# Two Mamba heads computed in pieces during attention's last blocks, and a hand-made order for the first units of the next layer

## The chip, the cores and the metric

The kernel runs on one core of a Trainium2 chip. The core has five engines that work side by side, each with its own instruction queue: TensorE (PE, matrix products; its weight loads are shown apart as PEld), VectorE (DVE), ScalarE (ACT), GpSimd (POOL) and SyncE (SP, which here only issues DMAs). An instruction starts when those ahead of it in its queue have started and the semaphores that it waits for have come. The metric is the device time of one execution in microseconds, the median of three runs.

## The reference

Four layers run over one image `x` of 2 x 64 channels x 96 x 96 pixels, L = 9216 pixels for each of two batch items.

```python
# layer 0: attention over all pixels, softmax not scaled
f = einsum('bnc,bcm->bnm', theta_x, phi_x)
y = einsum('bnm,bmc->bnc', softmax(f), g_x)
x = batchnorm(conv1x1(y)) + x
# layer 1: depthwise 3x1 and 1x3, 1x1 convolution, batch norm, relu,
#          then one Mamba over the L pixels of an item
seq = relu(bn(conv1x1(x + dwh(x) + dww(x))))
h = layernorm(seq)
xm, z = split(h @ in_proj.T)
xc = silu(causal_conv4(xm) + b)
dt, Bm, Cm = split(xc @ x_proj.T)          # 4, 16, 16
dt = softplus(dt @ dt_proj.T + dt_b)
h_t = exp(dt_t * A) * h_{t-1} + dt_t * B_t * xc_t     # 128 x 16 states
x = ((sum_s h_t C_t + xc * D) * silu(z)) @ out_proj.T + seq
# layer 2: four more Mambas along rows and columns, two directions each
# layer 3: a 3x3 filter made from the image's own channel means
```

Only the joint of layers 0 and 1 is touched.

## The kernel before

Channels lie on partitions: item 0 on rows 0 to 63, item 1 on 64 to 127. Two tiles, `xa` and `xb`, of 128 x 9216 float32 hold the image.

**Attention** is `layer0_direct`. For each item it makes `theta`, `phi` and `g` (the last in the lower half of `xb`) and then goes over 18 blocks of 512 queries, each in 18 groups of 512 keys. In a group PE makes two score tiles (`scores`, L302) while ACT turns the scores of that group into exponentials (`exps`, L316), PE multiplies those of the group before with `g` (`values`, L327), and DVE adds them up for the softmax's sums (L405, L414). Score tiles alternate between two PSUM buffers of two banks each (`f`); the banks `m` and `po` serve a block's `sums` (L349) and `project` (L362), which are done for the last block at groups 3 and 7 of the next. Small pieces of other work are hung into the groups by generators: weights of layer 1 in item 0 (`ready_weights`), and in item 1 the depthwise convolution of layer 1 (`convolution`, L192 and L201 on DVE), whose chunks of 768 pixels go to DRAM (`image1`, L183). It is done for eleven of twelve chunks. After the last block come `fold`, `sums`, `invert` and `project` with nothing beside them. Then a flag is loaded by all engines and a branch taken (L149): if a softmax sum was out of range, `layer0_general` does attention again in a safe form. In the measured runs it is skipped.

**Layers 1 and 2** are `layers1_2`. The scan over pixels is cut in units: 24 of layer 1 (2 items x 12 chunks of 768 pixels), then 96 of layer 2. A unit has a *head*: centring and layer norm (`norm_*`), the causal convolution with 4 taps (`conv`), the gate, Silu, the step width (`step_*`, which ends in four products that are summed by PE, `sum_mm`), and a write of step width and input to DRAM rows (`step_write`, L928). Then sixteen *steps*: 16 x 8 states of a group are spread over the partitions by DMA from those rows (`read`, L964, two DMAs of 384 KB each, into six buffers `spread`), ACT makes the decays (L987), DVE multiplies the inputs by B (L1000, into the PSUM tiles `place`) and scans (L1009 with a carried state in layer 1, L1014 in layer 2), POOL multiplies by C (L1016), PE gathers (L1027). C, B and the tail are further products. All products of heads and tails go through one pair of PSUM banks with tag `m` (`open`, `mm`), so that each must be read by ACT before the next may begin.

The order of all this is not left to a scheduler. The tables `CARRY` and `FRESH` give each operation a due time in steps, counted from its unit's first step, and `run` (L1211) sorts them all and issues them in that order, every engine's queue being filled in it. Units are 16 steps apart, and heads begin some 47 steps before their unit. The first unit is an exception: its head is issued whole at the start, together with the pointwise convolution of chunks 0 to 4 (`first`, L207 and L208), and the second unit is placed 32 steps after the first, one unit's length being left for its head:

```python
begin = self.STEPS * (i + (i > 0))
order += [(begin + when, u, name, args) for when, name, args in self.events(u) if i or not is_head((0, name))]
```

Before that, `layers1_2` issues all loads of the image chunks (L1272) and the depthwise convolution of the twelfth (L192, L201), from `xa`, which then becomes the room for small tables (`carver`). The pointwise convolutions of chunks 5 to 11 and the weights of layer 2 are made by a generator `other`, two of its pieces in each unit.

Of the kernel before, what the change touches and what calls it, by code (L numbers as in the profile page):

```python
# [19 lines left out]
FP = mybir.dt.float32  # L20
# [5 lines left out]
P = 128  # L26
B, C, H, W = 2, 64, 96, 96
L = H * W
# [44 lines left out]
def rows_of(b):  # L73
    return slice(b * C, (b + 1) * C)
# [62 lines left out]
    return scale, bias  # L137


def layer0(k, x, pre):  # L140

    nc, tc = k.nc, k.tc
    scale, bias = batch_norm(k, "bn0", "bn0_gamma", "bn0_beta", "bn0_mean", "bn0_var", "w_b")
    bad = layer0_direct(k, scale, bias, pre)
    with tc.If(nc.values_load(bad, min_val=0, max_val=1) > 0):  # L149
        nc.sync.dma_start(out=k.xa, in_=x)  # L150
        layer0_general(k, scale, bias)
        with tc.tile_pool(name="pre", bufs=2) as wp:
            for c in range(L // CH - 1):
                for _ in pre.chunk(c, wp):
                    pass


class Pre:
# [49 lines left out]
        self.nc.scalar.activation(part, whole, AF.Relu, bias=self.bias, scale=self.scale)  # L208


def layer0_direct(k, scale, bias, pre):


    nc, tc = k.nc, k.tc
# [6 lines left out]
    with (  # L221
# [121 lines left out]
        def fold(block):  # L343
            block.fold = wp.tile([P, NB], FP, tag="fold", bufs=1, name="fold")
            nc.gpsimd.tensor_add(block.fold, block.acc[:, :NB], block.acc[:, NB:])
# [24 lines left out]
        def convolutions():  # L370
            for c in range(L // CH - 1):
                while not ready or ready[-1] < pre.takes(c):
                    yield
                yield from pre.chunk(c, wp)

        ready_weights = prepare(k, att.tile([P, 640], FP, name="scratch"), product)
        convolution = convolutions()
        last = None
        for b in range(B):
            rows = rows_of(b)  # L380


            theta = att.tile([P, L], FP, tag="theta", name=f"theta{b}")
            phi = att.tile([P, L // 2], FP, tag="phi", name=f"phi{b}")
            g = k.xb[:, : KEYS * C].rearrange("p (m c) -> p m c", m=KEYS)


            sides = ((rows, k.xa[rows, : L // 2]), (rows_of(1 - b), k.xb[rows_of(1 - b), L // 2 :]))
            projections(theta, phi, g, sides)

            pending = None
            for i in range(NBLK):
                block = SimpleNamespace(rows=rows, i=i, acc=wp.tile([P, 2 * NB], FP, tag="acc", name="acc_e"))
                for n in range(NGROUP):
                    es = exps(scores(theta, phi, i, n))
                    if n == 3 and last:
                        sums(last)
                    if n == 7 and last:
                        project(last)
                        if last.rows == rows_of(B - 1):  # L400
                            ready.append((last.i + 1) * NB)
                    if n == 0:
                        nc.vector.tensor_add(block.acc, es[0], es[1])
                    else:
                        nc.vector.tensor_add(block.acc, block.acc, es[0])  # L405
                    if pending:
                        one, at, e = pending
                        if at == 0:
                            one.y = [bank("y0"), bank("y1")]
                        values(g, one.y, at, e)  # L410
                        if at == NGROUP - 1:
                            collect(one)
                    if n:
                        nc.vector.tensor_add(block.acc, block.acc, es[1])  # L414
                    if n == 0 and last:
                        fold(last)
                    if n == 3 and last:
                        invert(last)
                    pending = block, n, es
                    if b == 0 and (made or 5 <= n < NGROUP - 1):  # L420
                        made.clear()
                        next(ready_weights, None)
                    if b == B - 1:
                        next(convolution, None)
                last = block
            one, at, e = pending
            values(g, one.y, at, e)
            collect(one)
        fold(last)
        sums(last)  # L430
        invert(last)
        project(last)
        ready.append(L)
        for _ in convolution:
            pass
# [271 lines left out]
class Mamba:  # L707
# [37 lines left out]

    def open(self, name="mm"):

        return self.wide(self.ps_m.tile([P, 2 * NB], FP, tag="m", name=name))

    def half(self, sides, j, terms, rows=slice(0, P)):  # L750

# [37 lines left out]
    def norm_square(self, u):  # L789

        if u.carry:
            u.norm.x = self.work("xn", D_CONV - 1 + CH)
            u.sq = self.sq
            self.nc.scalar.activation(u.sq, u.p, AF.Square)
            self.nc.scalar.copy(u.norm.x[:, D_CONV - 1 :], u.p)  # L795
# [28 lines left out]
    def norm_scale(self, u):  # L824
        if u.norm.unit is not u:
            return
        nc = self.nc
        x = u.norm.x[:, D_CONV - 1 :]
        if u.carry:
            before = u.norm.x[:, : D_CONV - 1]  # L830
            if u.norm.before is None:
                nc.gpsimd.memset(before, 0.0)
            else:
                nc.gpsimd.tensor_copy(before, u.norm.before.x[:, CH:])
        nc.gpsimd.tensor_mul(x, x, u.sq)

    def norm_affine(self, u):
# [370 lines left out]
                add(s + table["shared"], "shared", *divmod(s // 4, PARTS))  # L1208
        return at

    def run(self, units, first, n_first, other, ending):  # L1211


        self.ending = (units[-1], ending)
        for u in units:
            u.dtu, u.h, u.decay, u.bx, u.C = {}, {}, {}, {}, {}
        self.nc.scalar.preload_act_table_set("natural_log_exp_and_others")
        first(0)
        heads = ("norm", "image", "conv", "gate", "silu", "step", "sum", "c")
        is_head = lambda e: e[1].split("_")[0] in heads  # L1220
        for _, name, args in sorted(filter(is_head, self.events(units[0])), key=lambda e: e[0]):
            getattr(self, name)(units[0], *args)
            if name == "norm_root":
                first(1)
            if name == "c_read_1":
                first(2)
        for c in range(3, n_first):
            first(c)
        order = []
        for i, u in enumerate(units):  # L1230
            begin = self.STEPS * (i + (i > 0))
            order += [(begin + when, u, name, args) for when, name, args in self.events(u) if i or not is_head((0, name))]
        for _, u, name, args in sorted(order, key=lambda e: e[0]):
            if name == "other":
                next(other, None)
            else:
                getattr(self, name)(u, *args)


def prepare(k, scratch_tile, product):  # L1240
# [9 lines left out]
    yield from mamba_weights(k, k.weights[0], k.const, product, 0)  # L1250


def layers1_2(k, pre, padded):

# [9 lines left out]
    with ExitStack() as stack:  # L1266
# [1 line left out]

        last = L // CH - 1
        FIRST = 5  # L1270
        for c in range(last):
            nc.sync.dma_start(out=k.xb[:, bass.ts(c, CH)], in_=pre.image[:, bass.ts(c, CH)])  # L1272

        for _ in pre.depthwise(last, k.xb[:, bass.ts(last, CH)]):
            pass

        def first(c):

            pre.pointwise(k.xb[:, bass.ts(c, CH)], *(m.places[c % 3] if c % 3 < 2 else m.open()))


        carver = Carver(k.xa)
        for _ in by_state(k, k.weights[0], carver, 0):
# [34 lines left out]

        def other():
            for c in range(FIRST, L // CH):  # L1320
                part = k.xb[:, bass.ts(c, CH)]
                sides, whole = m.open()
                for j, p in enumerate(sides):
                    rhs = part[:, bass.ts(j, HALF)]
                    nc.tensor.matmul(p, lhsT=k.mat("conv_w"), rhs=rhs, start=True, stop=True)
                yield
                nc.scalar.activation(part, whole, AF.Relu, bias=pre.bias, scale=pre.scale)
                yield
            for (which, lin_w, _), to in zip(layer2, joins):
                for i in which:  # L1330
                    yield from mamba_weights(k, k.weights[i], carver, m.product, i)
                yield from joined(which, lin_w, to)
# [17 lines left out]
        for (which, _, lin_b), to, order in zip(layer2, joins, ("p (t n) -> p n t", "p (n t) -> p n t")):  # L1350
            xs = k.xb.rearrange(order, n=W)
            for b in range(B):
                rows = rows_of(b)
                for n in range(0, W, SEQS):
# [12 lines left out]
                    pair[1].out.append((to[2][rows], half))  # L1367
                    pair[1].last, norm.unit = pair, pair[0]
                    units += pair
        m.run(units, first, FIRST, other(), padded.early)  # L1370


class Padded:
# [133 lines left out]
@with_exitstack  # L1507
def conv_seq_kernel(ctx: ExitStack, tc: tile.TileContext, x, cols, mats, dtw, out):
    k = setup(ctx, tc, x, cols, mats, dtw)
    dram = ctx.enter_context(tc.tile_pool(name="dram", bufs=1, space=bass.MemoryType.DRAM))  # L1510
    pre = Pre(k, dram)
    layer0(k, x, pre)
    padded = Padded(k)
    with tc.manual_schedule():
        layers1_2(k, pre, padded)
        layer3(k, padded, out)


# [79 lines left out]
```

## Time and profile before

| | us |
|---|---|
| runs | 7355.49, 7357.27, 7360.73 |
| median | 7357.27 |
| the profiled execution, its time | 7357.56 |
| its span | 7355.6 |
| last `y_one` copy of attention | 2378.99 |
| first operation after the branch | 2394.56 |
| one block of attention in item 1 | 64.18 |

| engine | busy us | share of the span |
|---|---|---|
| PE | 6315.5 | 86% |
| DVE | 6693.8 | 91% |
| ACT | 5484.4 | 75% |
| POOL | 4609.6 | 63% |

The page cuts the span into 40 slices of 184 us and gives each engine's busy share in tenths:

```profile
PE   9999999999999688887788778788787777777777
...
DVE  6788887888888499999999999999999999999999
ACT  5555555555555688887888888888888888888884
POOL 0000000000000489888899999999999999999996
PEclk9999999999999799999899999999999999999998
DMA  1000000000000466665677667677676766766764
```

A 9 is 90% or more. PEclk is the clock that PE was granted, in tenths of full speed. The fourteenth slice holds the joint of layers 0 and 1. In a timeline each line has a start, a busy time, the engine, the line of the code, the operation with its output and inputs, and how many instructions are merged; a bracket gives the idle time just before, and what ended it. A release is inferred from semaphores, and a wait for several is put down to the one that came last.

### The profile page before, as it was taken

To read this page: it belongs to the slowest core of one execution; us is meant where nothing else is said; L and a number is where in the kernel's file an instruction comes from. 1 tells how busy PE (TensorE), PEld (TensorE's weight loads), DVE (VectorE), ACT (ScalarE), POOL (GpSimd) and SP (SyncE) were. 2 spreads that over 40 slices of the span, in tenths; PEclk is the share of its full clock that TensorE was granted. 3 is DMA by queue.
4 is the path that set the end of the run, shared out by engine and by line. 5 is a ranking of instruction groups with operands and counts; after the bars stand their busy time and mean duration, and the time that the engine had idled before them with its cause. 6 is when DMAs were issued, how large, how long until landed. Compare 5 with 4: busy or idle time off the path is not lost.

```text
span 7355.6 us, 106020 instructions
## 1 busy us (share of the span) xinstructions
PE 6315.5 (86%) x38502; PEld 2351.6 (32%) x38502; DVE 6693.8 (91%) x5703; ACT 5484.4 (75%) x7902; POOL 4609.6 (63%) x3078
## 2 busy tenths in 40 slices
PE   9999999999999688887788778788787777777777
PEld 3333333333333233222233333233333333333333
DVE  6788887888888499999999999999999999999999
ACT  5555555555555688887888888888888888888884
POOL 0000000000000489888899999999999999999996
PEclk9999999999999799999899999999999999999998
DMA  1000000000000466665677667677676766766764
GB/s 47 1 1 1 1 1 1 3 6 6 6 6 6 123 163 169 164 170 155 176 182 183 180 178 183 176 184 181 181 183 177 185 182 175 187 182 176 186 180 129
DMA packets 301157, 878.11 MB, mean 119 GB/s; under 512 B 33608, under 2 KB 35660, under 8 KB 300112
## 3 DMA queue, kind: packets, MB, share of 16 engines
q1 hardware_dynamic: 300184, 869.94, 45.5%
q8 instruction: 303, 4.96, 0.3%
q14 instruction: 230, 1.88, 0.1%
q10 hardware_dynamic: 440, 1.32, 0.1%
HBM read 767.71 MB, written 103.42 MB: 118 GB/s over the span
## 4 chain that ended last, share of the span: by engine, by line
DVE 16%; issue 13%; PE 11%; ACT 7%; POOL 4%; DMA 2%; DVEq 0%; POOLq 0%; ACTq 0%; SPq 0%
DVE h L1014 9%; DVE place L1000 7%; PE mm L757 6%; POOL h L1016 3%; ACT h L987 2%; DMA spread<-rows 2%; PE conv L859 1%; PE y L1027 1%; PE B L992 1%; PE y L1022 1%; ACT raw L864 0%; DVE done L1487 0%; ACT raw L873 0%; ACT xa L821 0%; ACT raw L870 0%
## 5 line engine op out<-in xcount | busy, mean ns | idle before, releaser
L1016 POOL TENSOR_TENSOR h<-h,C 128x768 f32<-128x768 f32 x1920 | 3455.2, 1821 | 291.0 <-DVE h L1014 245.1
L1014 DVE TENSOR_TENSOR_SCAN h<-h,place 128x768 f32<-128x768 f32 x1344 | 2286.7, 1737 | 12.6
L316 ACT ACTIVATE e<-f_exp 128x1024 f32<-128x1024 f32 x1296 | 1257.8, 1022 | 984.7 <-PE f_exp L302 984.6
L987 ACT ACTIVATE h<-spread,rates 128x384 f32<-128x384 f32 x3408 | 1838.9, 606 | 10.8 <-DMA spread<-rows 9.1
L1000 DVE TENSOR_TENSOR place<-spread,B 128x768 f32<-128x768 f32 x1704 | 1546.0, 947 | 133.3 <-DMA spread<-rows 53.5
L1027 PE MATMUL y<-h,held 128*32 128x384 f32 x7680 | 1102.7, 514 | 380.7 <-POOL h L1016 379.9
L327 PE MATMUL y<-e,xb 64*64 64x512 f32 x10368 | 1232.1, 590 | 0.0
L302 PE MATMUL f_exp<-theta,phi 64*64 64x512 f32 x10368 | 1230.1, 589 | 2.0 <-DVE xb L287 1.4
L405 DVE TENSOR_TENSOR acc_e<-acc_e,e 128x1024 f32<-128x1024 f32 x612 | 771.3, 1260 | 298.1 <-ACT e L316 280.6
L341 POOL TENSOR_TENSOR ys<-ys,y_one 128x512 f32<-128x512 f32 x36 | 45.9, 1275 | 1455.9 <-DVE ys L340 1455.9
L414 DVE TENSOR_TENSOR acc_e<-acc_e,e 128x1024 f32<-128x1024 f32 x612 | 811.0, 1325 | 65.5 <-DVE acc_e L405 1.8
L992 PE MATMUL B<-raw,xa 128*128 128x384 f32 x960 | 490.4, 596 | 263.1 <-DVE place L1000 260.7
L1009 DVE TENSOR_TENSOR_SCAN h<-h,state,place 128x384 f32<-128x384 f32 x720 | 670.8, 991 | 2.4
L327 PEld LDWEIGHTS y<-e,xb 64*64 64x64 f32 x10368 | 393.7, 133 | 728.1 <-issue 722.7
L302 PEld LDWEIGHTS f_exp<-theta,phi 64*64 64x64 f32 x10368 | 395.3, 133 | 713.7 <-issue 701.9
L1027 PEld LDWEIGHTS y<-h,held 128*32 128x32 f32 x7680 | 212.6, 109 | 1151.9 <-POOL h L1016 761.8
L366 POOL TENSOR_TENSOR xa<-xa,t_att 64x512 f32<-64x512 f32 x36 | 54.5, 1514 | 756.6 <-ACT t_att L364 735.9
L757 PE MATMUL mm<-dtu,ident 128*128 128x384 f32 x960 | 427.1, 551 | 24.9 <-ACT xb L1065 14.5
L934 PE MATMUL mm<-raw,xa 128*128 128x384 f32 x960 | 376.2, 515 | 31.3 <-ACT xn L795 27.8
L1000 POOL TENSOR_TENSOR bx<-spread,xa 128x768 f32<-128x768 f32 x216 | 392.7, 1818 | 4.7 <-ACT xa L996 3.2
L992 PEld LDWEIGHTS B<-raw,xa 128*128 128x128 f32 x960 | 159.3, 207 | 578.2 <-DVE place L1000 412.6
L1014 DVE TENSOR_TENSOR_SCAN h<-place,bx 128x768 f32<-128x768 f32 x192 | 334.1, 1740 | 0.3 <-ACT place L987 0.3
(222 smaller groups left out, 7050.1 us busy)
## 6 DMA issues: line engine op xcount, KB each, us to landing
spread<-rows SPq DMA_DIRECT2D x1920, 384.0 KB, 6.1
rows<-dtu SPq DMA_DIRECT2D x120, 768.0 KB, 4.6
image<-pre SPq DMA_DIRECT2D x11, 384.0 KB, 2.3
xb<-image SPq DMA_DIRECT2D x11, 384.0 KB, 7.3
xa<-in_x SPq DMA_DIRECT2D x1, 2304.0 KB, 22.6
xa<-in_x SPq DMA_DIRECT2D x3, 384.0 KB, 11.3
xb<-in_x SPq DMA_DIRECT2D x3, 384.0 KB, 11.9
xa<-in_x SPq DMA_DIRECT2D x1, 1152.0 KB, 17.9
```

What stands on the lines that cost most here:

```text
L302: nc.tensor.matmul(f[rows_of(half), bass.ts(side, NB)], lhsT=phi[at, m * P + half * C : m * P + (half + 1) * C], rhs=theta[at, bass.ts(i, ...
L316: nc.scalar.activation(e, f, AF.Exp)
L327: nc.tensor.matmul(ys[half][rows_of(side)], lhsT=g[at, m, :], rhs=e[at, bass.ts(side, NB)], start=m < 2, stop=m >= KEYS - 2,)
L405: nc.vector.tensor_add(block.acc, block.acc, es[0])
L414: nc.vector.tensor_add(block.acc, block.acc, es[1])
L757: self.nc.tensor.matmul(o, lhsT=lhsT, rhs=x, start=n == 0, stop=n == len(terms) - 1)
L987: self.nc.scalar.activation(u.decay[step][:, q], dt[:, q], AF.Exp, scale=rate)
L992: self.nc.tensor.matmul(self.B, lhsT=u.w.bc[0][part], rhs=x, start=True, stop=True)
L1000: engine.tensor_mul(u.bx[step], self.spread(u, step, 1), B)
L1014: nc.vector.tensor_tensor_scan(*flat, 0.0, ALU.mult, ALU.add)
L1016: nc.gpsimd.tensor_mul(h, h, C)
L1027: self.nc.tensor.matmul(y, lhsT=self.t.gather[block // 4], rhs=u.h[step][:, q], start=False, stop=stop)
```

## The change

A new class `Early` computes the heads of the first two units of layer 1. Its generator `pieces` does pointwise convolution, layer norm, taps and gate for unit 0 and then unit 1, cut at each `yield`; `layer0_direct` takes a piece in each group from 9 to 16 of item 1's blocks from the fifth on, and further ones while a product is held in a bank (`yield True`). Products use the banks `m` and `po` by halves of 384 columns. The rest, Silu for both units and the step width of unit 0 up to its rows in DRAM, is issued between and after `fold`, `sums`, `invert` and `project`. Its tiles lie in the upper half of `xb`, which attention no longer needs in item 1. The branch's safe side does the same afterwards.

In `layers1_2` the chunk loads, the pointwise convolutions and the last chunk's depthwise convolution (`edge`) become events with due times, since the upper half of `xb` comes free only later. `run` leaves out the heads that are done, puts unit 1 at 2.5 steps behind unit 0's end (`GAPS`), gives the rest of its head times of its own (`SECOND`), and shortens the lead of unit 2's head by 0.85 (`FACTORS`). A new method `emit` walks the sorted events and holds one back while a tile or bank that it takes (`TAKES`) is not yet given back (`GIVES`). Eight products into an unread bank (`FILL_FIRST`) open the layer. A one-column Silu comes before the switch to the table set with Ln and Exp.

The diff, cut to its core:

```diff
+class Early:
...
+        for c, raw in enumerate(self.raw):
+            image, xc, gate = self.both[:, bass.ts(c, CH)], raw[:, :CH], raw[:, CH:]
...
+            nc.sync.dma_start(out=image, in_=pre.image[:, bass.ts(c, CH)])
+            yield
+            yield
+            ps = product(k.mat("conv_w"), image)
+            yield True
+            for j, p in ps:
+                nc.scalar.activation(part(image, j), p, AF.Relu, bias=pre.bias, scale=pre.scale)
+            yield
+            yield
+            ps = banks()
+            for j, p in ps:
+                nc.tensor.matmul(p, lhsT=k.tables.centre[own], rhs=part(image[own], j), start=True, stop=True)
+            yield True
...
+            for j, p in ps:
+                nc.scalar.activation(part(sq, j), p, AF.Square)
+                nc.scalar.copy(part(x, j), p)
+            yield
+            yield
+            ps = product(k.mean, sq, split=True)
+            yield True
+            for j, p in ps:
+                nc.scalar.activation(part(sq, j), p, AF.Ln, bias=k.eps)
+            nc.scalar.activation(sq, sq, AF.Exp, scale=-0.5)
+            yield
+            nc.gpsimd.tensor_mul(x, x, sq)
+            yield
+            nc.scalar.activation(x, x, AF.Identity, bias=k.col("ln_b"), scale=k.col("ln_g"))
...
+            yield self.REST if c else None
+        for raw in self.raw:
+            nc.scalar.activation(raw, raw, AF.Silu)
+        xc = self.raw[0][:, :CH]
+        nc.scalar.preload_act_table_set("natural_log_exp_and_others")
+        yield
+        ps = product(w.step, xc)
+        for j, p in ps:
+            nc.scalar.activation(e[:, j], p, AF.Abs, bias=w.dt_b)
+            nc.scalar.activation(dt[:, j], p, AF.Relu, bias=w.dt_b)
+        yield
+        nc.scalar.activation(e, e, AF.Exp, scale=-1.0)
+        nc.scalar.activation(kept, e, AF.Identity, bias=1.0)
+        nc.scalar.activation(kept, kept, AF.Identity, scale=-1.0, bias=1.0)
+        nc.scalar.activation(log, e, AF.Ln, bias=1.0)
...
+        nc.gpsimd.tensor_mul(e, dt, by_half(xc))
+        nc.sync.dma_start(out=self.rows, in_=self.both)
...
                     if b == B - 1:
                         next(convolution, None)
+                    if b == B - 1 and i >= 4 and held != Early.REST and (held or 9 <= n < NGROUP - 1):
+                        held = next(head, False)
...
         fold(last)
+        next(head)
         sums(last)
+        next(head)
         invert(last)
         project(last)
+        for _ in head:
+            pass
...
+        for i in range(self.fill):
+            self.nc.tensor.matmul(sides[i % 2], lhsT=k.ident, rhs=k.mats[:, :HALF], start=True, stop=True)
...
+    GAPS = (2.5, 0, 0)
+    FACTORS = (0.85, 1, 1)
...
+    FILL_FIRST = 8
+    FILL = 0
+    FILL_UNTIL = 3
+    LOADS = (-6.1, 2.3, 5.6, 8.7)
+    FIRST_1 = 11
...
         for i, u in enumerate(units):
-            begin = self.STEPS * (i + (i > 0))
-            order += [(begin + when, u, name, args) for when, name, args in self.events(u) if i or not is_head((0, name))]
+            begin = self.STEPS * i + sum(self.GAPS[:i])
...
+        for when, chunks in zip(self.LOADS, ((2,), (3,), (4, 0, 1), (5, 6, 7))):
+            when = min(when, *(firsts[c] - 1 for c in chunks if c in firsts), 100)
+            order.append((when, None, "load", load, chunks))
+        self.emit(sorted(order, key=lambda e: e[0]))
...
-        for c in range(last):
-            nc.sync.dma_start(out=k.xb[:, bass.ts(c, CH)], in_=pre.image[:, bass.ts(c, CH)])
-
-        for _ in pre.depthwise(last, k.xb[:, bass.ts(last, CH)]):
-            pass
...
             for c in range(FIRST, L // CH):
+                if c == FIRST + 1:
+                    load(8, 9)
+                if c == FIRST + 2:
+                    load(10)
+                    edge()
```

## The prediction

> **What bounds the kernel now.** I read the forty slices first: PE is at nine tenths up to about a third of the span, DVE from there to the end. The slices between are neither, and they are what the change touches. Stretches cut at the joints of the timeline give sizes:
>
> ```profile
> 2300.00:2350.00 50.00, 50.00 (x456) 17.38 (x452) 41.94 (x35) 28.54 (x30) 4.90 (x3) 1.00 0.00 1
> ...
> 2394.50:2453.00 58.50, 37.75 (x87) 16.61 (x88) 4.66 (x6) 27.98 (x35) 3.58 (x4) 0.70 0.38 119
> 2453.00:2496.40 43.40, 32.44 (x120) 12.88 (x122) 42.21 (x47) 33.30 (x51) 32.55 (x32) 0.73 0.45 104
> 2496.40:2533.00 36.60, 25.44 (x66) 9.48 (x62) 0.00 (x0) 16.89 (x20) 7.54 (x8) 0.72 0.61 151
> 2533.00:2576.40 43.40, 33.62 (x122) 13.57 (x122) 41.88 (x47) 35.96 (x57) 33.79 (x33) 0.80 0.53 137
> ```
>
> Columns: stretch, length, busy us of PE, weight load, DVE, ACT, POOL, granted clock, DMA share, GB/s. In attention PE has no idle time: work put there costs its full length. Then DVE works 4.7 us of 58.5 (unit 0's head is being made), 42 of 43.4 (unit 0), nothing for 36.6 (unit 1's head) and 42 of 43.4 again (unit 1). From there on DVE is about 98% busy (835 us of 2600 to 3450), so whatever brings the first two units forward reaches the end of the kernel. The timeline names the two stalls:
>
> ```profile
> 2382.39 1.13 PE L349 MATMUL m<-fold,ones 128*128 128x512 f32 x2 [3.49 <-POOL fold L345]
> ...
> 2389.82 0.77 ACT L364 ACTIVATE t_att<-po,bn_bias,bn_scale 64x512 f32<-64x512 f32 x1 [10.25 <-PE po L362]
> ...
> 2394.66 0.68 DVE L192 TENSOR_SCALAR xb<-xa,dw_centre,dw_b 128x768 f32<-128x768 f32 x1 [4.72 <-PEq L149]
> ...
> 2423.85 1.28 ACT L874 ACT_TABLE_LOAD   x1
> ...
> 2440.60 0.34 SPq L928 DMA_DIRECT2D rows<-dtu  x1
> ...
> 2452.97 1.83 DVE L1000 TENSOR_TENSOR place<-spread,B 128x768 f32<-128x768 f32 x2 [53.54 <-DMA spread<-rows]
> ...
> 2533.04 1.83 DVE L1000 TENSOR_TENSOR place<-spread,B 128x768 f32<-128x768 f32 x2 [36.69 <-PE B L992]
> ```
>
> **A. Pieces inside attention: +20 us.** Both heads up to the gate run in four or five of batch 1's blocks. Per unit PE gets five groups: pointwise (2 matmuls of 384 columns), centring (2, one row half, so one after the other), mean (2 halves side by side, as long as one), taps (8 in pairs, as 4), gate (as 1), together ten lengths. A length is about 0.64 us (L757 shows 0.81 for 2 records at full clock, of which the last part is drain). Each group also breaks attention's alternation. That price is in the trace: a block of 18 groups takes 64.18 us (distance of two L339 copies), a plain group 3.433, so the two inserted 512-column matmuls (L349, L362) cost 2.38, 1.19 each, of which 0.85 is streaming and 0.34 the break. Two units: 2 x (6.4 + 5 x 0.34) = 16.2 us, nothing beside it.
>
> ACT has 1.49 us idle of each 3.43 (the bracket before L316). In the timeline the pair of exps ends at 2373.18, and PE first needs their second bank again at 2374.43, 1.25 later, so ACT can take some 2.7 us more in one group before PE stalls. Relu, conv read, affine and gate (about 1.0 us each) and the squares and copies (about 1.9) fit. The root does not: two Ln halves (0.56 each, by the 384-column exps of L987), Exp 0.84, and two table loads, one to the set with Ln and one back. By the trace's row (1.28 us, the next ACTIVATE follows at once) that is 4.5 us, a stall of 1.8 per unit, 3.6 for both. The Trainium skill ("ScalarE: Activation LUTs", section "What ACT_TABLE_LOAD costs") says that a switch costs a drain of 1.38 us besides the 1.28 of the load. By it the root takes 7.3 us, stalls 4.5 per unit, and A is 25. The trace has no such gap around L873 and L874, so I take the row and keep 25 as the upper end; the lower end, no breaks and no stall, is 12.8. The two image loads in SP's queue are asked for two groups (6.9 us) before their matmul; an image write lands in 2.3 us alone. POOL is 8% busy there: its pieces cost nothing, and would cost only if later than their two groups.
>
> **B. Tail and unit 0: -32.5 us** (against 2452.97, without A's shift). After the last copy at 2379.6 ACT loads a table, does two Silus (1.48 each), loads back: 2385.2. PE does the sums first, then unit 0's step product, to 2386.4; Abs and Relu by halves end near 2387.5, under DVE's reciprocal and before `t_att` needs ACT (2389.8). So no cost to attention's own tail. Behind `t_att` (2390.6) come Exp, two Identities, Ln (3.4 us): 2394.0. The sums follow; the same tail, Ln's end to the last matmul, took 6.1 us before at the low clock: 2400. Copy 0.5, POOL product 1.8, rows write issued 2402.5; issue to the first read was 3.9 us before: 2406.4. The branch now stands behind all this on PE; its compare took 3.8 us after a 0.5 us load, so PE goes on at 2404.4 instead of 2394.6, beside the write.
>
> Two things now release unit 0's first DVE operation. Data: reads from 2406.4, with the small weights and one image load before them, first spread 6 to 8.5 us later, 2413 to 2415. PE: its new order puts eight filling matmuls, chunk 2's pointwise, unit 2's centring and unit 1's step product ahead of unit 0's B. The first clock-up row I see (L757, 2429.3 to 2435.4) shows 0.64 us a record for 6 us, then 0.33: filling 8.2 us. The Trainium skill ("TensorE: Matmul & The Clock Gate", section "What's actually happening") puts the ramp at one window of about 3.4 us: filling 6.9. I take the row: 2412.5, then 1.3 + relu 1.2 + 1.3 + two reads 1.6 + 1.3 + 0.8 for B, about 2420.5. ACT's three table loads (3.9 us), copies and dummy Silu end by 2410, under the filling. PE decides, not data: 2417 if PE stays warm, 2425 if cold.
>
> **C. Between units 0 and 1: -28.7 us.** The order asks for 2.5 steps of 2.71 (43.4 / 16), 6.8 us, in place of 36.7. Unit 1's rows write stands behind ten h products on POOL: 2420.5 + 27 + 3, its own 1.8 and issue give 2454; 4 us to land, 8.5 to the first spread: 2466. Unit 0 ends at 2464. On ACT, unit 0's stretch holds 32 exps (18 us) and about 21 us of heads; with unit 2's step chain (5.3) ahead of unit 1's first exps it ends near 2468. On PE, all products go through one bank pair `m`: thirteen groups at about 25 us of matmul, 15 of reads, 5 of handing over are 45 us. So a gap of 8 us; ends 3 and 20. SP's order puts images 4, 0, 1 and 5 to 7 ahead of unit 1's write: eight image loads beside eighteen transfers of the same size, so DMA near 0.65 x 26 / 18 = 0.94 of its time in unit 0; spreads have six buffers in hand, so I add nothing but keep the upper end for it.
>
> **D. Depthwise of the last chunk: +4.75 us.** L192 and four L201 ran while DVE was idle (2394.66 to 2399.43). They now stand between two scans of the third unit, where nothing hides them. Ends 3 and 5.
>
> **E. Heads of units 2 to 4 are begun later relative to PE and ACT work: +2 us**, by the 1.9 us that DVE was idle in 2600 to 2650; 0 to 10. The `other` steps are the same steps, one unit later: nothing. The added waits of the planner's hold rule act on order only, not on an engine.
>
> Sum: 19.8 - 32.5 - 28.7 + 4.75 + 2 = -34.7. The profiled execution took 7357.6 (span 7355.6), 0.3 above the median 7357.3: **7323 us**.
>
> **Rivals.**
> 1. Unit 1's head still comes late (the single `m` pair, where PE and ACT take turns, or DMA at 0.94). For it: PE had 0.73 of full clock in unit 0, and a 45 us chain does not fit 43.4 us at that clock. Against: twenty us of it were moved out. Gap 20 and E 8: 7341.
> 2. Attention takes the pieces better than I price them and PE stays warm: A 13, B -36, gap 3: -36 - 33.7 + 13 + 4.75 + 1 gives 7307. For it: ACT, POOL and DVE all have room. Against: the 0.34 us breaks are measured.
> 3. Slower: PE is in order, and a piece's matmul that waits for its ACT or DMA input stops attention altogether, since scores and values queue behind it. Each of 34 pieces would have to cost 34.7 / 34, 1.02 us, beyond A before the gain is gone; at half a group (1.7 us) each the time is 7381. Against: operands are made two groups ahead.
> 4. The pieces don't fit the window and run after attention: the order shows both heads ahead of the last blocks, so only a per cent or so.
>
> **Numbers.** Forecast 0.62 (own range 7308 to 7338), rival 1 0.17, rival 2 0.15, rivals 3 and 4 0.06. Bounds of A, C and E together give 7303 to 7348. What can be told from no change is 0.2%, 14.7 us: faster means under 7342.6. Forecast and rival 2 give 0.77 less 0.01, rival 1 half of its share and a bit: faster 0.88, same 0.07, slower 0.05.
>
> **What would show it.** Block distance of the y_one copies up from 64.18 to about 69 in four blocks (A). First place of layer 1 some 13 us earlier on the clock with A in it, behind B on PE rather than behind a spread (B). DVE idle between units 0 and 1 about 8 us (C). L197 and L206 between scans (D). It is wrong if the ACT exps of attention come after the table loads by far more than 2 us, if unit 1's first place waits over 15 us, or if later units show idle DVE.

## The result, and the profile after

| | before | after |
|---|---|---|
| median, us | 7358.6 (7355.49 to 7361.49) | 7332.58 (7329.32 to 7334.59) |
| span of the profiled execution, us | 7355.6 | 7329.6 |

Six runs each. The ratio is 0.9964, with an interval of 0.9954 to 0.9974: 26.0 us less, where 34.7 were forecast. The spans of the two profiled executions also differ by 26.0, so the traces may be compared term by term; each is a single execution, and how far a term moves between executions is said where it matters.

The page of the kernel after, its 40 slices of 183 us:

```profile
PE   9999999999999778887788878888787777777777
...
DVE  6787877887888699999999999999999999999999
ACT  5555555555555688887888888888888888888884
POOL 0000000010000588898999999999999999999996
PEclk9999999999999899998999999999999999999998
DMA  1000000000000566666766766766766766767764
```

Only the fourteenth slice stands out: DVE is at 6 there instead of 4. The stretches of the joint, cut as before (stretch, length, busy us of PE, weight load, DVE, ACT, POOL, granted clock, DMA share, GB/s):

```profile
2399.50:2442.67 43.17, 29.06 (x54) 12.88 (x54) 6.69 (x7) 23.44 (x33) 5.55 (x4) 0.72 0.31 87
2442.67:2491.35 48.68, 32.36 (x118) 14.00 (x122) 42.46 (x47) 34.93 (x53) 34.55 (x34) 0.89 0.73 197
2491.35:2500.80 9.45, 8.50 (x44) 3.52 (x36) 0.00 (x0) 6.35 (x10) 2.14 (x3) 1.00 1.04 239
2500.80:2547.10 46.30, 36.30 (x145) 14.08 (x146) 42.16 (x48) 37.85 (x58) 35.90 (x34) 0.96 0.53 136
```

The head of unit 0 takes 43 us behind attention instead of 74, and the gap between units 0 and 1 is 9.45 us instead of 36.6. But the units have grown: 48.68 and 46.30 us, where they took 43.4 and 43.7 with the same 42 us of work on DVE. So DVE now waits inside them.

The last `y_one` copy, at 2378.99 before, came at 2399.31. In seven profiles of the same attention, of this kernel and of runs below, it came between 2396.6 and 2401.3, so the joint is counted from this copy, not from the start of the span:

| term | how it is read off | predicted | measured |
|---|---|---|---|
| A | shift of the last `y_one` copy | +19.8 | +20.3 |
| B | copy to the first `place` of unit 0: 73.98 to 43.36 | -32.5 | -30.6 |
| C | first `place` of unit 0 to that of unit 2: 123.81 to 104.43 | -28.7 | -19.4 |
| D | the last chunk's depthwise, L197 and L206 | +4.75 | +9.0 |
| E | the rest, to the end | +2 | -5.3 |
| sum | | -34.7 | -26.0 |

**D**, in the timeline of DVE after:

```profile
2597.46 2.10 DVE L197 TENSOR_SCALAR xb<-xa,dw_centre,dw_b 128x768 f32<-128x768 f32 x1
2599.59 6.93 DVE L206 SCALAR_TENSOR_TENSOR xb<-xa,cols,xb 128x768 f32<-128x768 f32 x4
```

Before, the same five instructions took 0.68 and 4.06 us. What had changed is their company, in the timeline of POOL after:

```profile
2597.32 1.82 POOL L1157 TENSOR_TENSOR h<-h,C 128x768 f32<-128x768 f32 x1
2599.08 0.52 POOL L1151 COPY state<-h 128x2 f32<-128x2 f32 x1
2599.68 2.60 POOL L1157 TENSOR_TENSOR h<-h,C 128x768 f32<-128x768 f32 x1
2602.24 2.42 POOL L1178 TENSOR_TENSOR yg<-yg,raw 128x768 f32<-128x768 f32 x1
```

Both engines are stretched: the POOL product from 1.82 to 2.60, the copy from 0.19 to 0.52. L197 begins 0.13 us after a POOL product began and ends 0.42 us after that product's end. Taken singly, the four L206 took 1.02, 2.35, 2.44 and 1.01 us: the two long ones are those that began while a POOL product was under way.

**C**, in the timeline of DVE after (the bracket is the wait just before):

```profile
2468.05 1.83 DVE L1141 TENSOR_TENSOR place<-spread,B 128x768 f32<-128x768 f32 x2 [4.30 <-PE B L1133]
...
2489.43 1.92 DVE L1150 TENSOR_TENSOR_SCAN h<-h,state,place 128x384 f32<-128x384 f32 x2 [1.68 <-issue]
2500.80 1.83 DVE L1141 TENSOR_TENSOR place<-spread,B 128x768 f32<-128x768 f32 x2 [9.45 <-PE B L1133]
...
2513.18 1.93 DVE L1150 TENSOR_TENSOR_SCAN h<-place,state,bx 128x384 f32<-128x384 f32 x2 [4.04 <-ACT place L1128]
```

Four waits, 19.5 us. The one at the joint ends with a B product; the timeline of PE after shows what stood ahead of it:

```profile
2492.52 0.91 PE L897 MATMUL mm<-dtu,ident 128*128 128x384 f32 x2
2494.27 0.91 PE L897 MATMUL mm<-kept,ident 128*128 128x384 f32 x2 [0.84 <-ACT kept L1039]
2495.02 0.90 PE L897 MATMUL mm<-log,ident 128*128 128x384 f32 x2
...
2499.07 0.85 PE L1168 MATMUL y<-h,held 128*32 128x384 f32 x8
2499.85 0.91 PE L1133 MATMUL B<-xb,xa 128*128 128x384 f32 x2
```

The sums of unit 2's step head, which PE makes as ACT delivers their inputs, come first in PE's queue; B needs nothing but its turn.

Two theories follow. *Order*: single operations stand in front of more urgent ones, and each can be put behind them for its full wait. *Bank pair*: all products of heads and tails share the pair `m`, each turn running from the first product's write to the end of ACT's last read, and the pair is nearly always taken, so a better order would only move the wait. I worked the turns out from the PE and ACT rows of the trace: from 2431 to 2547.1, 28 turns hold the pair for 105.3 of 116.1 us, 91%; from 2431 to 2500, 93%. (The first 2 us are the end of the filling and the wait behind it.) A third theory is the low *clock* of PE in unit 0 (0.89).

### The profile page after: what moved, and what is told of

It reads as the page before. It is cut to its first block, busy times and chain, and to the rows that moved or that the text cites. A ratio compares the mean times of both kernels' runs of the same rounds, so it can differ in the third digit from the quotient of the medians.

```text
span 7329.6 us, 106080 instructions
## 1 busy us (share of the span) xinstructions
PE 6297.5 (86%) x38526; PEld 2345.8 (32%) x38526; DVE 6698.9 (91%) x5703; ACT 5492.1 (75%) x7924; POOL 4614.8 (63%) x3080
## 4 chain that ended last, share of the span: by engine, by line
DVE 17%; issue 13%; PE 11%; ACT 7%; POOL 3%; DMA 2%; DVEq 0%; SPq 0%; ACTq 0%; POOLq 0%
DVE h L1155 9%; DVE place L1141 7%; PE mm L897 6%; ACT h L1128 2%; POOL h L1157 2%; DMA spread<-rows 2%; PE B L1133 1%; PE y L1168 1%; PE conv L1000 1%; PE y L1163 1%; ACT xa L962 0%; ACT xa L963 0%; DVE done L1765 0%; ACT raw L1005 0%; ACT raw L1011 0%
## 5 line engine op out<-in xcount | busy, mean ns | idle before, releaser
L1155 DVE TENSOR_TENSOR_SCAN h<-h,place 128x768 f32<-128x768 f32 x1344 | 2286.2, 1736 | 12.7
L1128 ACT ACTIVATE h<-spread,rates 128x384 f32<-128x384 f32 x3408 | 1839.6, 606 | 10.6 <-DMA spread<-rows 9.1
L483 POOL TENSOR_TENSOR xa<-xa,t_att 64x512 f32<-64x512 f32 x36 | 54.7, 1520 | 757.6 <-ACT t_att L481 736.9
```

What stands on the lines that cost most here:

```text
L1128: self.nc.scalar.activation(u.decay[step][:, q], dt[:, q], AF.Exp, scale=rate)
L1155: nc.vector.tensor_tensor_scan(*flat, 0.0, ALU.mult, ALU.add)
```

## The experiments

"Less than after" subtracts medians. The kernel before, run again beside each set, had medians of 7358.6 to 7360.0, so a difference of 1 or 2 us says nothing by itself.

**The depthwise in attention's tail.** The last chunk is convolved behind the flag, while DVE has nothing else, and loaded as the others are.

```diff
-            for c in range(L // CH - 1):
+            for c in range(L // CH):
...
-        ready.append(L)
-        for _ in convolution:
-            pass
...
+        ready.append(L)
+        for _ in convolution:
+            pass
         return bad[:1]
...
-                    load(10)
-                    edge()
+                    load(10, 11)
```

> The last chunk's five depthwise operations are moved from the third unit to the end of attention (after the flag is made), stored to DRAM like the other eleven chunks and loaded with chunk 10. Theory (POOL beside them doubles them, 9.0 us between two scans): about 9 us less than the changed kernel (profiled span 7329.6, so about 7321), and each of the five back at 0.7 to 1.0 us, since POOL does one operation there. Rival (their price is 4.75 us as forecast, the rest was waiting that comes back elsewhere): 4 to 5 us less. Second rival (later idle time of DVE takes it up anyway): no difference.

Median 7323.4, ratio 0.9954 (0.9938 to 0.9971): 9.2 us less than after. The intervals overlap, and medians alone would not tell 9 from 4.75; the trace does: from the first `place` of unit 3 to that of unit 4 it took 42.15 us, and 51.13 after. So all 9.0 that the rows between the scans had shown went. The timeline of DVE in this run:

```profile
2411.03 0.68 DVE L197 TENSOR_SCALAR pre<-xa,dw_centre,dw_b 128x768 f32<-128x768 f32 x1 [2.10 <-POOL xa L483]
2411.74 4.06 DVE L206 SCALAR_TENSOR_TENSOR pre<-xa,cols,pre 128x768 f32<-128x768 f32 x4
```

The same instructions, with POOL idle, take 4.74 us again.

**One table set in attention.** The set with both Ln and Exp is loaded ahead of attention, so the root of a piece needs no switch.

```diff
+        nc.scalar.preload_act_table_set("natural_log_exp_and_others")
         ones = att.tile([P, P], FP, name="ones")
```

> The table set that has both Exp and Ln is loaded once, before attention's first Exp, so the four table loads of the two root pieces go. Theory (load 1.28 us each by the trace, 1.8 us of PE stall per unit): the two long blocks with a root go from 70.85 to about 69.0 us, 3.6 us less in all. Rival by the page's 2.66 us a switch: 4.5 us per block, 9 in all. Second rival (PE does not stall on the root): block distances stay at 70.85.

Each of the two long blocks fell from 70.85 to 69.08 us, 3.5 us together; the median was 7330.33, ratio 0.9962 (0.9947 to 0.9976), 2.3 less than after, which the intervals alone could not tell from nothing. The timeline of ACT in the kernel after shows the two loads that went:

```profile
1725.40 1.28 ACT L279 ACT_TABLE_LOAD   x1
1726.70 0.58 ACT L279 ACTIVATE head<-m,eps 128x384 f32<-128x384 f32 x1
1727.17 0.57 ACT L279 ACTIVATE head<-po,eps 128x384 f32<-128x384 f32 x1
1727.77 1.28 ACT L280 ACT_TABLE_LOAD   x1
1729.06 0.84 ACT L280 ACTIVATE head<-head 128x768 f32<-128x768 f32 x1
```

The function that follows a load starts 0.01 to 0.02 us after it ends. The stall of 1.8 per unit that was worked out from the row was the price, and it is gone.

**B ahead of the sums.** Against the wait of 4.30 in unit 0.

```diff
-        sum_mm_0=5.74,
+        sum_mm_0=6.25,
```

> Unit 0's third B product is put ahead of unit 1's first sums in PE's queue, nothing else. Order theory: DVE's wait of 4.30 us at step 8 of unit 0 goes. Whether time goes with it tells two things apart: if the chain of unit 2's Silu, step width and sums sets unit 1's start (chain theory), unit 0 ends 4 us earlier, the gap grows from 9.45 to about 13.5 and the total is the same within 1 us; if waits simply add up (sum theory), the total is 4 us less.

The 4.30 went, but DVE then waited 1.17, 3.8, 9.2, 4.04, 3.0 and 0.71. Unit 1 began 101.28 us behind the last copy (after: 101.49), unit 2 at 150.66 (after: 147.79), and the median was 7333.02, ratio 0.9964 (0.995 to 0.9978): no change.

**Unit 1's first products earlier.** Against the gap of 9.45: the first B product of unit 1 and its first two pairs of decays go ahead of unit 2's sums.

```diff
+    FIRST_STEPS = {
+        ("shared", (0, 0)): 15.6,
+        ("room", (0,)): 14.4,
+        ("decay", (0,)): 14.41,
+        ("room", (1,)): 15.29,
+        ("decay", (1,)): 15.3,
+    }
...
+                if i == 1:
+                    when = self.FIRST_STEPS.get((name, args), when)
```

> Unit 1's first B product and its first two pairs of decays are put ahead of unit 2's sums and logarithm in the queues of PE and ACT. Theory (unit 1's start stands behind unit 2's head in two in-order queues): the gap of 9.45 us falls to 1 to 3, what is left being the spread reads; 6 to 8 us less, if the 4.0 us wait at step 3 does not grow. Rival (the spread DMAs, at 1.04 of DMA time in the gap, set the start): the gap stays above 7 us and the wait is on DMA.

The timeline of DVE in this run:

```profile
2490.28 1.83 DVE L1141 TENSOR_TENSOR place<-spread,B 128x768 f32<-128x768 f32 x2 [1.95 <-PE B L1133]
...
2503.58 0.96 DVE L1141 TENSOR_TENSOR place<-spread,B 128x768 f32<-128x768 f32 x1 [7.84 <-ACT xa L1137]
...
2511.21 1.92 DVE L1150 TENSOR_TENSOR_SCAN h<-place,state,bx 128x384 f32<-128x384 f32 x2 [4.64 <-issue]
```

The gap fell to 1.95, and 7.84 appeared one operation later. Unit 2 began 148.5 us behind the copy (after: 147.79), and the median was 7337.87, ratio 0.9972 (0.9961 to 0.9984). No 6 to 8 us came of it: putting this wait's operations first did not gain its length. The rival of this run, that the DMAs of the spreads set the start, falls too, since the start moved. The 4.04 in unit 1 is the one wait that no run took away: it was 4.0 to 4.7 us in every run. Its decays stand in ACT's queue behind the read of a centring turn, and putting them ahead was not tested.

**Two pointwise convolutions later.** Those of chunks 0 and 1 in unit 0 are due ten steps later.

```diff
-    FIRST_1 = 11
+    FIRST_1 = 21
```

> The pointwise convolutions of chunks 0 and 1 (two turns on the single product bank pair, 5.3 us from 2479.0 to 2484.3 in the changed kernel, just ahead of unit 2's Silu) are due ten steps later, at step 21, nothing else. Chain theory (unit 1's start is set by a chain of turns between PE and ACT on the one bank pair, not by the order alone): unit 2's Silu follows its gate read at once, and unit 1's first place comes about 5 us earlier, counted from attention's last copy (96 instead of 101.5); 2 to 5 us less at unit 2's start, since the two turns come back in unit 1. Rival (spread DMAs set unit 1's start): the first place stays at 101 and the wait names DMA.

Unit 1 began 5.6 us earlier, 95.87 behind the copy, as expected of two turns fewer ahead of it. Unit 2 began at 149.75, 2.0 later than after: the two turns were only postponed. Median 7333.03, ratio 0.9963 (0.9949 to 0.9977).

**Rows written from ACT's queue.** ACT makes the last copies of unit 0's rows in the tail and would save a hand-over to SP.

```diff
-        nc.sync.dma_start(out=self.rows, in_=self.both)
+        nc.scalar.dma_start(out=self.rows, in_=self.both)
```

> Unit 0's rows are written from ACT's DMA queue instead of SP's, so that SP's jump (3.8 us, from 2424.9 to 2428.7 in the changed kernel, after the write's issue) is taken earlier. Theory (SP's jump is on the path of the first reads and of chunk 2's load): first place 1 to 2 us earlier from attention's last copy (43.4 there, 42 here), limited by PE's own chain of filling, pointwise, centring, step product and B. Rival (PE's chain alone sets it): no change within the scatter of 0.9 us between profiles.

Slower: median 7338.4 in nine runs, ratio 0.997 (0.996 to 0.998), the first `place` 45.67 us behind the copy instead of 43.36. The reads themselves went out 1.2 us earlier, as expected (30.03 us behind the copy, after: 31.20). But PE came out of the branch later. The first product behind it in the kernel after, and ACT's semaphore behind its own branch (a row of L149 has the durations in ns, then the start):

```profile
2424.73 7.12 PE L887 MATMUL mm<-mats,ident 128*128 128x384 f32 x16 [3.26 <-ACTq L149]
L149 ACTq EVENT_SEMAPHORE  x1: 17/17/17, 2424.7 to 2424.7; - x1
```

The same in this run, with ACT's write:

```profile
2423.64 0.36 ACTq L325 DMA_DIRECT2D rows<-xb  x1
L149 ACTq EVENT_SEMAPHORE  x1: 17/17/17, 2428.1 to 2428.1; - x1
2428.21 7.30 PE L887 MATMUL mm<-mats,ident 128*128 128x384 f32 x16 [7.42 <-ACTq L149]
```

Both times PE starts 0.06 to 0.07 us after ACT's semaphore, so it waits for ACT to come through. The write has to wait for POOL's product of the rows, which ends at 2423.61, and in ACT's queue it stands ahead of ACT's own branch. So ACT's compare came at 2424.57 in place of 2422.05, ACT was through at 2428.14 in place of 2424.67, and PE with it.

**Filling through unit 0.** Products into an unread bank keep PE busy, two at a time up to step 18.

```diff
-    FILL = 0
-    FILL_UNTIL = 3
+    FILL = 2
+    FILL_UNTIL = 18
```

> Two filling products are put ahead of every bank pair opened in unit 0 (FILL 2 instead of 0, until step 18 instead of 3). Clock theory (the low clock of PE makes the sums of unit 1 last 5 us and so delays B): the granted clock from the first place to unit 1 goes from 0.89 to 1.0, the wait at step 8 falls by 2 us or more, unit 1 starts earlier. Chain theory: each filling stands in the same in-order queue and costs 1.3 us per turn, some 15 turns before unit 1: unit 1's start 5 to 15 us later.

The granted clock was 1.00 from the first `place` to the end of unit 0 (stretches of this run, columns as above):

```profile
2441.84:2496.50 54.66, 44.83 (x170) 20.32 (x170) 42.45 (x47) 35.79 (x55) 34.56 (x34) 1.00 0.65 184
```

Yet this unit took 54.7 us, unit 2 began 10.1 us later than after, and the median was 7345.67, ratio 0.998 (0.9973 to 0.9988). The pair `m` was held 97% of the time. The filling stands in PE's queue too (44.83 us busy against 32.36), so the run doesn't show that the clock is worth nothing; it shows that a full clock bought this way doesn't pay. Against the clock as the cause of the waits speaks that unit 0 before took 43.4 us at a granted clock of 0.73.

**No filling at all.**

```diff
-    FILL_FIRST = 8
+    FILL_FIRST = 0
```

> The eight filling products at layer 1's start are left out. Clock theory: PE then starts chunk 2's pointwise at the low clock, the first turns (pointwise, centring, step product, B) take 0.64 us a record instead of 0.33, and unit 0's first place comes 3 to 5 us later (46 to 48 from attention's last copy instead of 43.4). Rival (PE waits for chunk 2's image until 2433.0 anyway, and the turns are mostly hand-overs): within 1.5 us of 43.4, the filling bought nothing.

Median 7332.68 in four runs of 7329.81 to 7342.1, ratio 0.9962 (0.9946 to 0.9977): the same as after. In the trace unit 0 and unit 2 begin some 2.2 to 2.5 us later, counted from the copy. But with the filling, and with the way through the branch unchanged, the first `place` already came anywhere from 42.8 to 44.5 us behind the copy, against 45.84 here. Whether the eight products are worth those 2 us, these runs can't tell.

**Two turns less.** Here the turns of chunks 0 and 1 are not moved but removed. Their pointwise convolution had already been made once by the pieces in attention; the result is written back in place of the chunk, and unit 0 doesn't make it again.

```diff
+            nc.sync.dma_start(out=pre.image[:, bass.ts(c, CH)], in_=image)
...
-        pointwise(self.FIRST_1, 0, 1)
```

> The pieces in attention make the pointwise result of chunks 0 and 1 anyway and overwrite it. Here it is written back to DRAM in place of its input, so that the two pointwise convolutions of chunks 0 and 1 in unit 0 are not done again: two turns of 2.6 us each on the product bank pair less, nothing else. Bank theory (from layer 1's first product to unit 2's start the one bank pair is held 91% of the time, and DVE's idle time of about 20 us in units 0 and 1 is what is left over, wherever the order puts it): unit 2's start moves 4 to 5 us earlier, counted from attention's last copy (147.8 to about 143), and DVE's idle time in units 0 and 1 falls from 19.5 to about 15. Order theory (which instruction stands behind which decides, and moving things moved it only by accident): the idle time stays at 19 to 22. Rival (unit 0's own spread reads and DMA): no change, waits name DMA.

Unit 2 began 143.79 us behind the copy, 4.0 earlier than after. Median 7326.0, ratio 0.9954 (0.9939 to 0.9969), 6.6 us less than after. The turns of `m`, worked out in the same way from about the end of the filling to the start of unit 2:

| run | turns | pair held, us | unit 2's start behind the copy |
|---|---|---|---|
| after | 28 | 105.3 | 147.79 |
| unit 1's products earlier | 28 | 104.3 | 148.5 |
| pointwise later | 27 | 106.5 | 149.75 |
| two turns less | 25 | 101.2 | 143.79 |

In the runs that only reorder, the pair is held about as long as in the kernel after and unit 2 begins no earlier. Where 4.1 us of holding go, unit 2 begins 4.0 earlier. That is clear of scatter: in after and in the runs of the depthwise and of the table set, which keep the order of units 0 to 2, unit 2 began 147.2 to 148.1 us behind the copy.

How far does this carry? It shows that turns removed bring time where the three moves of single operations brought none. It doesn't show the pair alone to be the limit. A turn's holding includes its waits for PE or ACT, and the pair is held for some 90% of the stretch in all four rows, so a longer stretch has more holding of itself. With the two turns went also 3.1 us of products on PE (2 x 1.56) and 2.0 us of reads on ACT (2 x 0.99), and either queue alone may be worth part of the 4.0. Nor do the two figures agree always so well: with one table set, where the order of layer 1 is that of after, the pair was held 2.0 us less (counted without the filling) and unit 2 began 0.55 earlier.

**Combinations.** The first put together the depthwise in the tail, one table set, the later pointwise and the rows from ACT.

> The parts that are expected to gain, together: depthwise of the last chunk at attention's end, one table set, the two pointwise convolutions later, unit 0's rows from ACT's queue. Sum of the parts (9.0 + 3.6 + 3 + 1): about 16 us less than the changed kernel, profiled span near 7313, a ratio of about 0.994 to the kernel before. Rival (the later layers give back what the start gains, since spans scatter by some 4 us after unit 2): 10 us or less.

It reached 7329.45, ratio 0.9958 (0.9941 to 0.9974), 3 us less than after instead of 16. Its first `place` came 46.37 us and unit 2 153.75 us behind the copy: the rows from ACT and the postponed turns took 6.0 us back of the 12.7 that the other two gave. The second had the depthwise in the tail, one table set and two turns less:

> Two turns less on the bank pair, one table set in attention, and the last chunk's depthwise convolution at attention's end, together. By the parts (4.5 + 3.6 + 9.0): 17 us less than the changed kernel, near 7315, a ratio of 0.994 to the kernel before. If later layers give back part: 12 us or less.

Median 7316.66 (7312.13 to 7321.44), ratio 0.9941 (0.9927 to 0.9954), 15.9 us less than after and the fastest version here. The single gains add up to 9.2 + 3.5 + 4.0 = 16.7, the first by medians, the others by their stretch of the trace; by medians alone they are 9.2 + 2.3 + 6.6 = 18.1. Stretches of its units 0 and 1 and the gap between them:

```profile
2439.66:2485.81 46.15, 32.56 (x122) 13.58 (x122) 42.23 (x47) 36.42 (x55) 34.17 (x34) 0.85 0.65 186
2485.81:2491.85 6.04, 6.04 (x26) 2.76 (x24) 0.00 (x1) 3.01 (x6) 2.40 (x4) 1.00 1.04 242
2491.85:2539.39 47.54, 37.67 (x140) 14.78 (x144) 42.47 (x47) 37.00 (x56) 36.37 (x35) 0.89 0.62 163
```

Still some 13 us more than two units of 43.4. A second pair of banks for these products would be the next thing, and would part the pair from the two queues; it wasn't tried.

## Why the prediction was right, and where it was not

The direction, the place of each term and most of A and B were right; the gain was 8.7 us smaller than forecast, halfway to the first rival (7341), whose mechanism, turns on the pair `m`, is the one that the runs point to.

**A, +20.3 for +19.8.** The distances of the `y_one` copies were 67.47, 70.85, 67.53 and 70.85 where 64.18 had stood, 20.0 in all; the other 0.3 of the shift lies outside these blocks. The short blocks have pointwise and centring, 2 x (1.28 + 0.34) = 3.24 by the prediction's prices, 3.29 and 3.35 measured; the long ones have mean, taps, gate and the root's stall, 2 x 0.98 + 2.9 + 1.8 = 6.66, and 6.67 measured. The choice of the row over the page held. The Trainium skill's 2.66 us a switch ("ScalarE: Activation LUTs", section "What ACT_TABLE_LOAD costs") would by the prediction's estimate have made 4.5 us of stall in each long block; taking the switches out brought 1.77. So the third rival, in which attention's in-order PE waits for the pieces, did not come.

**B, -30.6 for -32.5.** The last sum of the tail ended at 2421.47, which is 2401.1 without the shift of A, for 2400; the filling began at 2424.73, 2404.4 without it, the very time that was worked out. The way there was another, and the agreement is luck. PE's own compare, to which the prediction gave 3.8 us behind the sums, was over by 2419.3, under them; PE then waited until ACT was through at 2424.67, as shown above.

The step that failed in the data's path is that reads go out 3.9 us after the rows write. The timeline of SP after:

```profile
2424.33 0.33 SPq L325 DMA_DIRECT2D rows<-xb  x1
2429.29 0.34 SPq L1555 DMA_DIRECT2D xa<-in_dtw  x1
2429.82 0.34 SPq L1541 DMA_DIRECT2D xb<-image  x1
2430.51 3.98 SPq L1105 DMA_DIRECT2D spread<-rows  x6
```

It took 6.2 us. The branch is the reason: it now stands between SP's write and SP's reads. SP's compare came at 2424.7 and its last semaphore before the next DMA at 2428.7. "PE decides, not data" held by a hair: B ended at 2442.48 and a spread is named for the start at 2442.67, but in nine of the eleven runs above the same wait ends with B. From the end of the filling to B's end PE took 10.6 us, where the sum had 8. It waited 1.16 us for chunk 2's image, which SP asks for only behind its branch, and the step product and B took 2.39 and 1.49 us for 1.3 and 0.8, at a granted clock of 0.58. Filling took 7.12 us, nearer to the 6.9 that the prediction estimated from the skill's page than to the 8.2 of my row, and returned part of it.

**C, -19.4 for -28.7: the step that was mis-sized.** The gap itself came near, 9.45 for 8; but the prediction's own sums give it 2 to 7 us, so the nearness is in part luck. What the sum had left out is that units 0 and 1 no longer take 43.4 us: they took 5.3 and 2.6 us more, in waits inside them. The prediction had written the cause down, all products through one pair `m`, and set 45 us of turns against unit 0's 43.4 alone, then let that one difference be hidden by the gap. Eleven turns that begin in unit 0 did hold the pair 44.7 us, but from unit 0's first `place` to unit 2's it is 93.6 of 104.4 us, against the 87 us that DVE's work on two units took before: the deficit goes on through unit 1. The cause is shown as far as the run with two turns less shows it, with its limits. DMA, the other reason for the upper end of 20, had a share of 0.73 in unit 0, not 0.94, though 1.04 in the gap.

**D, +9.0 for +4.75.** Mis-sized by taking the time of instructions that ran alone. The Trainium skill ("SBUF — State Buffer", section "SBUF: two separate sides") says that DVE and GpSimd have a port pair in common: of a DVE instruction with two SBUF inputs and a GpSimd instruction that reads SBUF, the one that starts first holds it to its end, and the other blocks. The rows of L206 and of POOL agree with that. It speaks against this part of the change, and I hadn't weighed it. The profile before held the sign of it: `acc_e` additions of 1.23 us taking 2.1 beside a POOL addition. POOL is at 8 tenths in the slice where the five instructions were put, so a longer time was to be had from there.

**E, -5.3 for +2.** In the two profiles the later units lost nothing: from unit 2 to 3700 us, DVE's waits over 0.3 us came to 14.9 us, after 20.25 before. But one profile each doesn't carry the sign. In the eight runs above that leave the depthwise where it is, the rest behind unit 2's start took 4783.3 to 4789.0 us, 4782.5 after and 4778.9 before, so that E, less the 9.0 of D, lies anywhere from -5.3 to +1.1, and the profile after gives the lowest of all. What can be said is that the +2 did not show; why is open.

A and B left 2.4 us of the forecast unfulfilled, C and D 13.6, and E returned 7.3, which is within what it moves by between executions.

## What to carry to other kernels

Where products share one buffer and the engines hand it to and fro, add up how long it is held over the whole stretch, not its gap alone. Here that sum exceeded the bound engine's work; three reorderings then moved the wait, and only turns removed brought time. A vector instruction that is moved from an idle place to one beside a busy GpSimd has to be priced by a row that already ran in such company. And when a jump's cost is hidden on one engine, look at which queue pays it next.

## What the runs showed of the hardware

- DVE beside POOL: five fp32 instructions of 768 columns took 9.0 us between two scans with POOL busy, and 4.74 with POOL idle; one POOL product went from 1.82 to 2.60.
- The branch: SP needed 4.0 us from its compare to its last semaphore ahead of the next DMA. PE's first product behind it started 0.06 to 0.07 us after ACT's semaphore in all runs with the filling, so one DMA that moved from SP's queue to ACT's, ahead of ACT's branch, made PE come out 3.5 us later.
- A granted clock of 1.00 through unit 0, in place of 0.89, together with 12.5 us more of PE work, made the kernel 13 us slower.
